# A megakernel of a dynamic filter and a bidirectional Mamba block: TensorE's products of the scan path are placed one phase earlier in its order, and a gated product one scan later

## The chip, the core and the metric

One core of a Trainium2 chip runs the whole program in one launch. The metric is device time in microseconds (us); lower is better. All data is fp32 except for a few small bf16 selections.

The engines are called as in the profile: PE is TensorE (matmul), PEld its weight loads, DVE is VectorE, ACT is ScalarE, POOL is GpSimd and SP is SyncE, which here only issues DMAs.

## The reference, cut to what matters

Eight images of 64 channels and 128 x 128 pixels pass through two layers.

```python
# layer 0, "front": a filter of 3 x 3 taps predicted for each pixel
h = leaky_relu(conv3x3(x, w1) + b1)
w_lp = softmax(conv1x1(h, w2) + b2, axis=1)          # 9 weights a pixel
x = x + sum_k shift_k(x) * (delta_center - w_lp)[k]
# layer 1
x_norm = layernorm(x);  seq = layernorm(x_norm as 16384 tokens of 64);  res = seq
for l in range(2):                                    # two bidirectional Mamba blocks
    xin, z = in_proj(rmsnorm(seq))                    # 128 channels each
    for d in (forward, backward):
        u  = silu(causal_conv1d(xin)); dt = softplus(dt_proj(x_proj(u)))
        h_t = exp(dt * A) * h_{t-1} + dt * u * B      # 128 channels x 16 states
        y_d = sum_n(C * h) + D * u
    seq = seq + out_proj((y_f + y_b) * silu(z))
# "mix"
x = x + dwconv(conv1x1(x_norm)) * (conv3x3(rmsnorm(seq)) + res)
# "ffn"
g1, g2 = dwconv(conv1x1(layernorm(x)))                # 170 channels each
x = x + conv1x1(gelu(g1) * g2)
```

## The kernel before, in words

The selective scan is the long part: 128 channels x 16 states = 2048 independent recurrences over 16384 tokens, twice (two directions) for each of two layers and eight images. A **chunk** is 1024 tokens of one direction of one layer of one image; a chunk has U = 16 scan **steps**, each of which does the recurrence of 128 rows (32 channels x 4 states) over 1024 tokens. 8 images x 64 chunks x 16 steps make 8192 scans, which run one after the other on DVE. For each of these steps:

- POOL forms `bu` = (dt x u) x B for two steps at a time (`drive`, L991, three buffers).
- ACT forms the decay exp(dt x A) in PSUM, two steps ahead (`decay`, L999, tile `w`, two buffers).
- DVE scans (`scan`, L1017 and L1019) and, in about two thirds of the steps, multiplies by C (`product`, L1041); in the others POOL does (L1038).
- ACT saves the last column as the next chunk's start (`keep`, L1031), and PE sums the states into `y` (`collect`, L1050 and L1057, one buffer).

The work that feeds a chunk runs one to two chunks ahead, as methods of the class `Chunk`; PE's part of it is what the text calls the **main path's products**: `conv` (L869, tile `xp`, read by ACT L875 into `xc`), `gate` (L884, `zp`, ACT L892), `step` (L910, `dp`, ACT L917 into `dt`), `bc` (L928, `bcp`, ACT L935), and after a backward-and-forward pair `project` (L1086 and L1089, `op`), a norm's `means` (L405, `ms`) and `spread` (L420, `rb`, read by DVE L1103 in `normed`). All of them write one PSUM tag, `mm`, with one buffer: each has to wait until the one before it has been read.

Beside the scans run, spread over the steps, the three per-image stages `Front`, `Mix` and `Ffn` (the **side work**), with PSUM tags `bg` and `acc` of one buffer each. While one image's 1024 steps run, steps 0 to 180 or so have the Mix of the image before beside them, 180 to 569 its Ffn, and 569 to 1024 the Front of the next image. After the last scan comes the last image's Ffn, alone.

The order of every engine's instructions is written out by hand. Each method is filed under a pair (time in steps, phase), and the pairs are worked off in sorted order, methods of one pair in the order in which they were filed, chunks before Front, Mix and Ffn. A method issues its instructions on its engine's queue there and then, and each engine goes through its queue in that order.

```python
FEED, SCAN, MID, PROD, DECAY, REST = range(6)
def at(time, phase, fn, *args):
    steps.setdefault((time, phase), []).append((fn, args))
...
for key in sorted(steps):
    for fn, args in steps[key]:
        fn(*args)
```

So inside one step FEED comes first, then the scan, its product, then DECAY (where all evacuations of PSUM stand) and at last REST (where most of PE's side work stands). A main path product filed under FEED of step t follows all that is filed under REST of step t-1.

In Ffn, `gelus` (L763 for `gt`, L765 for `ga`, on ACT) is filed at a + 11 under REST; a table load for gelu goes ahead of it and one for exp follows it. `rest_times` (L768, DVE) multiplies `gt` by the other half in PSUM.

Of the kernel before, what the change touches and what calls it, by code (L numbers as in the profile page):

```python
# [36 lines left out]
FEED, SCAN, MID, PROD, DECAY, REST = range(6)  # L37
# [18 lines left out]
def kernel(ctx: ExitStack, tc: tile.TileContext, a: dict, out: bass.AP):  # L56
# [123 lines left out]
    with tc.tile_pool(name="wspill", bufs=1) as fp, tc.tile_pool(name="wprep", bufs=2) as pp, \  # L180
# [98 lines left out]
        for l in range(DEPTH):  # L279
# [17 lines left out]
            for d in range(2):  # L297
                cw = pp.tile([DI, KC], F32, tag="cw", name="cw")
                nc.sync.dma_start(cw, a["L1_conv_conv_w"][l, d])
                for j in range(KC):  # L300
                    t = turned(inx2, diagonal(cw[:, j : j + 1], DI), P, DI)
                    at = j if d == 0 else KC - 1 - j
# [51 lines left out]
    def at(time, phase, fn, *args):  # L354
        steps.setdefault((time, phase), []).append((fn, args))
# [349 lines left out]
    class Ffn:  # L705
# [92 lines left out]
        def plan(self, a):  # L798
            early = 12 if self.alone else 0
            at(a - 4 - early, REST, self.load, 0)  # L800
            at(a - 3 - early, REST, self.load, 1)

            if self.alone:
                groups = ((0, 0, self.first_out, 2), (3, 2, None, 0), (6, 1, self.times, 9))
                gelus, out = 5, 12
            else:
                groups = ((0, 0, self.first_out, 5), (6, 2, None, 0), (14, 1, self.times, 19))
                gelus, out = GELU, 19
            for t, g, end, to in groups:
                for i in range(4):  # L810
                    at(a + t + (0 if self.alone else i), REST, self.conv, g, i)
                for h in range(2 if end else 0):
                    at(a + to, DECAY, end, h)
            at(a + gelus, REST, self.gelus)
            at(a + gelus + 1, DECAY, self.rest_times)
            at(a + out - 5, REST, self.load_x2)
            at(a + out, REST, self.project)
            at(a + out + 2, DECAY, self.add)
            at(a + out + 2, REST, self.store)
# [15 lines left out]
    class Chunk:  # L835
# [282 lines left out]
        def plan(self):  # L1118
            b = self.t0 - 2 * U
            at(b + 3, REST, self.load_hn)  # L1120
            for h in range(2):
                at(b + 7 + h, FEED, self.conv, h)
                at(b + 7 + h, DECAY, self.conv_out, h)
                if self.second:
                    at(b + 9 + h, FEED, self.gate, h)
                    at(b + 9 + h, DECAY, self.gate_out, h)
                at(b + 14 + h, FEED, self.step, h)
                at(b + 14 + h, DECAY, self.step_out, h)
            at(b + SILU, REST, self.silu)
            at(b + SOFTPLUS, REST, self.softplus)  # L1130
            if self.second:
                at(b + 13, REST, self.store_gate)
            b = self.t0
            at(b - 16, FEED, self.bc)
            at(b - 16, DECAY, self.bc_out)
            at(b - 14, REST, self.store_bc)
            at(b - 13, REST, self.store_dt)
            at(b - 11, FEED, self.dtx)
            at(b - 10, REST, self.store_du)
            j0 = self.pairs[0][0] // 2  # L1140
            at(b - 10, REST, self.load_states, "bp", j0)
            at(b - 8, REST, self.load_channels, "dup", 0)
            at(b - 6, REST, self.load_channels, "dtp", 0)
            at(b - 5, REST, self.load_states, "bp", 1 - j0)
            at(b - 4, REST, self.load_channels, "dup", 1)
            at(b - 4, REST, self.load_states, "cp", j0)
            at(b - 2, REST, self.load_channels, "dtp", 1)
            at(b + 0, REST, self.load_states, "cp", 1 - j0)
            for k in range(U // 2):
                at(b + 2 * k - 5, REST, self.drive, k)  # L1150
                at(b + 2 * k + 3 + (k % 4 == 0), REST, self.collect, k)
            for u in range(U):
                at(b + u - 2, DECAY, self.decay, u)
                at(b + u, SCAN, self.scan, u)
                at(b + u + self.on_pool(u), FEED if self.on_pool(u) else PROD, self.product, u)
            for h in range(2):
                if self.second:
                    at(b + 8 * h + 1, REST, self.load_yf, h)
                    at(b + 8 * h + 6, REST, self.add_yf)
                    at(b + 8 * h + 7, REST, self.load_gate, h)  # L1160
                if self.second:
                    at(b + 8 * h + 12, FEED, self.y_out, h)
                else:
                    at(b + 8 * h + 11, DECAY, self.y_out, h)
                    at(b + 8 * h + 12, REST, self.store_y, h)
            if not self.second:
                return
            b += U
            n = self.norm
            at(b + 2, REST, self.load_h)  # L1170
            at(b + 5, FEED, self.project)
            at(b + 6, DECAY, self.residual)
            at(b + 6, DECAY, self.square)
            if self.l == 0:
                at(b + 7, REST, self.store_h)
            at(b + 12, FEED, lambda: n.means(mm_tile, self.sq))
            at(b + 13, DECAY, n.means_out)
            at(b + 14, REST, n.root)
            at(b + 17, FEED, n.spread, mm_tile)
            at(b + 18, DECAY, self.normed)  # L1180
            if self.l:
                at(b + 19, DECAY, self.weighted)
            at(b + 19, REST, self.store_hn)
# [7 lines left out]
    for b in range(B):  # L1191
        a, last = IMAGE * b, b == B - 1
# [36 lines left out]
```

## Time and profile before

| | us |
|---|---|
| median of 3 timed runs (30005.71 to 30014.66) | 30010.1 |
| time of the profiled execution | 29956.31 |
| its span from first to last instruction | 29954.4 |
| before the first scan | 579.7 |
| from the first scan's start to the last scan's end | 28757.6 |
| after the last scan | 617.2 |

Mean granted TensorE clock over the span: 0.881. The fourth image's 1024 steps, cut into the three stretches in which Mix, Ffn and Front stand beside the scans (busy time of each engine, from the table by stage):

| stretch (us from the span's start) | us | PE | DVE | ACT | POOL | granted clock |
|---|---|---|---|---|---|---|
| 11417.10 to 12044.00, Mix | 626.90 | 519.94 | 577.58 | 385.87 | 601.53 | 0.88 |
| 12044.00 to 13385.40, Ffn | 1341.40 | 1126.44 | 1258.54 | 878.22 | 1261.76 | 0.91 |
| 13385.40 to 15029.70, Front | 1644.30 | 1350.96 | 1539.39 | 1054.05 | 1601.07 | 0.88 |

Idle time of an engine is the stretch less its busy time. The list of waits puts the idle time just ahead of an instruction down to what released it: "who <- whom: us in total, times, longest us". In the timeline a line is: start, length, engine, line of the kernel, operation, tiles, shape, count, and in brackets the idle time before it and its releaser.

### The profile page before, as it was taken

How to read it: one execution, taken by the hardware profiler on the slowest of the kernel's cores; microseconds unless marked ns; L12 is line 12 of the kernel's file. 1: busy time of each engine (PE TensorE's matmuls, PEld its weight loads, DVE VectorE, ACT ScalarE, POOL GpSimd, SP SyncE). 2: the span in 40 equal slices, each digit the busy share in tenths (PEclk: the TensorE clock that was granted, in tenths of full speed). 3: DMA queues.
4: the chain of work that ended last, by engine and by line, in shares of the span. 5: the costliest groups of instructions: out<-in, count | busy, mean ns of one | idle time of the engine just before them, and what ended most of it. 6: DMA issues, size and time to landing. Idle time of an engine off the chain costs nothing. (4 is left out here: it accounts for less than half of the span.)

```text
span 29954.4 us, 307972 instructions
## 1 busy us (share of the span) xinstructions
PE 24257.7 (81%) x96344; PEld 8093.1 (27%) x96344; DVE 27086.6 (90%) x17258; ACT 18533.8 (62%) x28316; POOL 27661.8 (92%) x8732
## 2 busy tenths in 40 slices
PE   7666888878888788887888788887888878888579
PEld 3211232223322233222322223222232223322123
DVE  3899999999999999999999999999999999999992
ACT  2566666666666666666666666666666666666661
POOL 3999999999999999999999999999999999999991
PEclk8777888988989888988899889898898988889789
DMA  4776676766777677776777767776677766777672
GB/s 100 210 241 214 221 235 230 237 213 223 237 231 237 213 225 237 232 232 210 233 232 238 225 214 232 232 237 223 215 236 232 240 214 222 235 234 234 214 240 75
DMA packets 2529698, 6617.29 MB, mean 221 GB/s; under 512 B 417862, under 2 KB 722262, under 8 KB 2525750
## 3 DMA queue, kind: packets, MB, share of 16 engines
q1 hardware_dynamic: 2528054, 6597.59, 68.4%
q8 instruction: 761, 12.47, 0.2%
q14 instruction: 883, 7.23, 0.1%
HBM read 5363.40 MB, written 1266.10 MB: 221 GB/s over the span
## 5 line engine op out<-in xcount | busy, mean ns | idle before, releaser
L991 POOL TENSOR_TENSOR bu<-dup,bp 128x2048 f32<-128x2048 f32 x4096 | 18578.8, 4539 | 557.7 <-DVE w L1019 421.4
L999 ACT ACTIVATE w<-dtp,a_neg 128x1024 f32<-128x1024 f32 x8192 | 9162.3, 1118 | 510.2 <-DVE hs L1017 313.9
L1038 POOL TENSOR_TENSOR hs<-hs,cp 128x1024 f32<-128x1024 f32 x2832 | 6685.3, 2361 | 197.9 <-ACT state L1031 133.3
L1041 DVE TENSOR_TENSOR hs<-w,cp 128x1024 f32<-128x1024 f32 x5360 | 6564.9, 1225 | 310.9 <-DMA cp<-bc_dram 77.6
L1017 DVE TENSOR_TENSOR_SCAN w<-w,state,bu 128x1024 f32<-128x1024 f32 x2677 | 6280.9, 2346 | 346.5 <-ACT w L999 345.9
L1019 DVE TENSOR_TENSOR_SCAN w<-w,state,bu 128x1024 f32<-128x1024 f32 x2683 | 6291.0, 2345 | 314.1 <-ACT w L999 313.5
L1057 PE MATMUL y<-hs,sel_y 128*32 128x512 f32 x32768 | 5183.3, 702 | 33.0 <-POOL hs L1038 32.6
L1031 ACT COPY state<-w 128x1 f32<-128x1 f32 x5360 | 837.4, 156 | 5040.0 <-DVE hs L1041 5004.5
L1017 DVE TENSOR_TENSOR_SCAN hs<-w,state,bu 128x1024 f32<-128x1024 f32 x1419 | 3321.3, 2341 | 86.4 <-ACT w L999 36.9
L1019 DVE TENSOR_TENSOR_SCAN hs<-w,state,bu 128x1024 f32<-128x1024 f32 x1413 | 3307.7, 2341 | 52.8 <-ACT w L999 34.7
L1050 PE MATMUL y<-xc,dskip 128*64 128x512 f32 x4096 | 1622.3, 860 | 2025.6 <-ACT yv L1074 1339.3
L869 PE MATMUL xp<-hn,wx 128*128 128x512 f32 x4096 | 2269.2, 682 | 485.3 <-ACT xc L875 339.8
L746 PE MATMUL fp<-fw,bgw 128*128 128x512 f32 (+1 forms) x6144 | 2353.9, 638 | 64.7 <-ACT ga L759 63.5
L1057 PEld LDWEIGHTS y<-hs,sel_y 128*32 128x32 f32 x32768 | 736.8, 116 | 3496.6 <-issue 2469.7
L1031 ACT COPY state<-hs 128x1 f32<-128x1 f32 x2832 | 540.2, 191 | 1829.2 <-DVE hs L1019 929.6
L414 POOL TENSOR_TENSOR r<-r,neg_half 128x8 f32<-128x8 f32 x768 | 1263.5, 1645 | 380.5 <-ACT r L411 323.9
L875 ACT ACTIVATE xc<-xp,cbias 128x512 f32<-128x512 f32 x1024 | 697.2, 681 | 1415.1 <-PE xp L869 1414.7
L910 PE MATMUL dp<-xc,wdt 128*128 128x512 f32 x2048 | 1228.5, 684 | 351.8 <-ACT dt L917 268.2
L752 PE MATMUL fp<-fw,bgw 64*128 64x512 f32 (+1 forms) x6144 | 1501.1, 608 | 0.0
L999 ACT ACT_TABLE_LOAD x1134 | 1454.9, 1283 | 20.1
L947 POOL TENSOR_TENSOR dt<-dt,xc 128x1024 f32<-128x1024 f32 x512 | 1212.8, 2369 | 246.5 <-DMA dt_dram<-dt 223.8
L510 PE MATMUL acc<-t,ident 128*128 128x512 f32 x2304 | 1361.3, 675 | 0.0
(184 smaller groups left out, 26903.7 us busy)
## 6 DMA issues: line engine op xcount, KB each, us to landing
bp<-bc_dram SPq DMA_DIRECT2D x4096, 256.0 KB, 4.0
dup<-du_dram SPq DMA_DIRECT2D x4096, 256.0 KB, 5.0
dtp<-dt_dram SPq DMA_DIRECT2D x4096, 256.0 KB, 5.0
cp<-bc_dram SPq DMA_DIRECT2D x4096, 256.0 KB, 5.0
hn<-hn_dram SPq DMA_DIRECT2D x1024, 256.5 KB, 4.8
dt_dram<-dt SPq DMA_DIRECT2D x512, 512.0 KB, 3.1
du_dram<-dt SPq DMA_DIRECT2D x512, 512.0 KB, 2.6
yf_dram<-yv SPq DMA_DIRECT2D x512, 256.0 KB, 4.4
```

The costliest lines, as they stand in the source:

```text
L746: nc.tensor.matmul(o, wpair[:, i, g, m], self.win[h][:, i : i + ROWS, 0:W], start=(i == 0), stop=False)
L752: nc.tensor.matmul(o, wlast[rows, i, g, m], self.win[h][rows, i : i + ROWS, lo : W + lo], start=False, stop=(i == 2),)
L869: nc.tensor.matmul(self.xp[h], wx[:, self.l, self.d, i, :], self.hn2[:, s.start + 2 * i : s.stop + 2 * i], start=(i == 0), stop=(i == 1),)
L991: nc.gpsimd.tensor_tensor(bu, self.dup[self.pairs[k][1]], self.over_pair("bp", k), ALU.mult)
L999: nc.scalar.activation(w, self.dtp[gp][:, i, :], AF.Exp, scale=a_neg[:, self.l, self.d, g, j : j + 1])
L1017: nc.vector.tensor_tensor_scan(to, w, bu, s0, ALU.mult, ALU.add)
L1019: nc.vector.tensor_tensor_scan(to[:, ::-1], w[:, ::-1], bu[:, ::-1], s0, ALU.mult, ALU.add)
L1031: nc.scalar.copy(self.column(u), h[:, T - 1 : T] if self.d == 0 else h[:, 0:1])
L1038: nc.gpsimd.tensor_tensor(hs, hs, c, ALU.mult)
L1041: nc.vector.tensor_tensor(hs, w, c, ALU.mult)
L1050: nc.tensor.matmul(self.y[C * h : C * h + C, :], dskip[:, self.l, self.d, C * gp : C * gp + C], self.xc[:, s], start=True, stop=False,)
L1057: nc.tensor.matmul(self.y[lo : lo + 32, :], sel_y, hs[:, i, s], start=False, stop=(k % 4 == 3))
```

## The change

Every main path product goes from FEED of step t to REST of step t-1. Within REST of one step chunks are filed first, so these products then stand on PE ahead of the Front, Mix and Ffn products of REST of step t-1, and no longer behind them; `project` also passes the `collect` of the following chunk that opens a new `y`. What is filed under DECAY (all reads of these products) stays. `dtx` and `y_out`, on POOL and DVE, stay under FEED. `rest_times` goes from DECAY of the step after the gelus to MID of the step after that: behind one more scan. While the last image's Ffn runs alone, there is no scan between, and DVE's order is the same there.

The order of the instructions changes on PE, and on DVE in 112 places (seven images x 16 tiles), where `gt` L768 and the scan that followed it change places. On ACT, POOL and SP it stays the same, instruction for instruction.

```diff
@@ Ffn.plan
             at(a + gelus, REST, self.gelus)
-            at(a + gelus + 1, DECAY, self.rest_times)
+            at(a + gelus + 2, MID, self.rest_times)
@@ Chunk.plan
             b = self.t0 - 2 * U
             at(b + 3, REST, self.load_hn)
             for h in range(2):
-                at(b + 7 + h, FEED, self.conv, h)
+                at(b + 6 + h, REST, self.conv, h)
                 at(b + 7 + h, DECAY, self.conv_out, h)
                 if self.second:
-                    at(b + 9 + h, FEED, self.gate, h)
+                    at(b + 8 + h, REST, self.gate, h)
                     at(b + 9 + h, DECAY, self.gate_out, h)
-                at(b + 14 + h, FEED, self.step, h)
+                at(b + 13 + h, REST, self.step, h)
                 at(b + 14 + h, DECAY, self.step_out, h)
...
             b = self.t0
-            at(b - 16, FEED, self.bc)
+            at(b - 17, REST, self.bc)
             at(b - 16, DECAY, self.bc_out)
...
             b += U
             at(b + 2, REST, self.load_h)
-            at(b + 5, FEED, self.project)
+            at(b + 4, REST, self.project)
             at(b + 6, DECAY, self.residual)
             at(b + 6, DECAY, self.square)
...
-            at(b + 12, FEED, lambda: n.means(mm_tile, self.sq))
+            at(b + 11, REST, lambda: n.means(mm_tile, self.sq))
             at(b + 13, DECAY, n.means_out)
             at(b + 14, REST, n.root)
-            at(b + 17, FEED, n.spread, mm_tile)
+            at(b + 16, REST, n.spread, mm_tile)
             at(b + 18, DECAY, self.normed)
```

## The prediction

> **What bounds the kernel now.** The page's busy line first:
>
> ```profile
> PE 24257.7 (81%) x96344; PEld 8093.1 (27%) x96344; DVE 27086.6 (90%) x17258; ACT 18533.8 (62%) x28316; POOL 27661.8 (92%) x8732
> ```
>
> POOL and DVE are both nearly full, so the question is which of the two waits for the other. In DVE's list of waits, taken up to the end of the last scan (29337 us), no row has POOL's `bu` as releaser:
>
> ```profile
> DVE w L1017 <- ACT w L999: 345.9, 302, 3.2
> DVE hc L529 <- PE rb L420: 321.8, 127, 15.7
> DVE w L1019 <- ACT w L999: 313.5, 193, 3.2
> DVE t L504 <- PE wb L500: 199.7, 103, 11.1
> DVE gt L768 <- ACT gt L763: 171.8, 107, 2.2
> DVE hn L561 <- PE rb L420: 141.7, 70, 14.4
> DVE hn L1103 <- PE rb L420: 134.7, 79, 3.7
> ```
>
> POOL does wait for DVE (`bu` <- DVE w L1019 421.4 us, L1017 116.3 us), and in the timeline of the fourth image its `bu` ends on average 4 to 11 us before its scan starts. DVE sets the pace, POOL follows with little to spare: by the table by stage its idle time per image is 25.4 us beside Mix, 79.6 beside Ffn and 43.2 beside Front, 148 in all. A microsecond that DVE no longer waits is time, as long as POOL keeps up.
>
> DVE waits for ACT's decay, though ACT is busy for 62%. ACT's list says why:
>
> ```profile
> ACT xc L875 <- PE xp L869: 1414.7, 634, 18.3
> ...
> ACT dt L917 <- PE dp L910: 526.8, 294, 4.6
> ACT bc L935 <- PE bcp L928: 509.5, 249, 3.8
> ```
>
> ACT works in order; while it waits for a main path product, the next decay stands behind. One such place in the timeline (step 11 of a chunk, beside Ffn):
>
> ```profile
> 12383.97 1.98 PE L869 MATMUL xp<-hn,wx 128*128 128x512 f32 x4
> ...
> 12385.99 0.69 ACT L875 ACTIVATE xc<-xp,cbias 128x512 f32<-128x512 f32 x1 [3.04 <-PE xp L869]
> ...
> 12386.61 1.13 ACT L999 ACTIVATE w<-dtp,a_neg 128x1024 f32<-128x1024 f32 x1
> ...
> 12387.78 2.36 DVE L1019 TENSOR_TENSOR_SCAN w<-w,state,bu 128x1024 f32<-128x1024 f32 x1 [2.39 <-ACT w L999]
> ```
>
> PE was late because eight Ffn products (12382.05, 1.99 us) stood ahead of xp; the buffer had been free since 12381.85. And the gelu wait:
>
> ```profile
> 9629.52 0.69 DVE L768 TENSOR_TENSOR gt<-gt,fp 128x512 f32<-128x512 f32 x1 [1.52 <-ACT gt L763]
> ...
> 9631.88 1.12 ACT L999 ACTIVATE w<-dtp,a_neg 128x1024 f32<-128x1024 f32 x1
> ...
> 9633.65 2.34 DVE L1019 TENSOR_TENSOR_SCAN hs<-w,state,bu 128x1024 f32<-128x1024 f32 x1
> ```
>
> **Part A, the gated product.** 112 times `gt` goes behind a scan of 2.35 us. DVE waits 171.8 us there now (the page's 528.4 less 356.6 in the tail, where order and wait stay), at most 2.2 us at a time, so the scan covers it; its own decay is ready in every case. Next is late the scan after that: its decay stands on ACT behind the gelus and a table load, ends at 9633.00 in the rows above and was needed at 9633.65. This margin of 0.65 us is the same at nearly all 112 places, so if ACT's times stay, only min(wait, 0.6) is won, summed 60 us. ACT comes to the gelus after a `conv_out` or `step_out` that waits for PE (2.78 us in this example); where part B takes 1 us of that away, the whole 172 us is won. I take 140, with ends 60 and 172. What queues behind the later `gt` is one product L1041, 0.7 us later; its PSUM buffer is next written 7 us after (9637.42).
>
> **Part B, main path products earlier.** No instruction is added, no DMA moves, SP's and POOL's queues are passed by nothing. 2590 us of ACT's idle time stand before reads of these products (the three rows above and 140.6 for `gate`), but only what reaches DVE counts. DVE's rows with ACT w as releaser are 345.9 + 313.5 + 36.9 + 34.7 = 731 us. I went through them by step: step 11 alone has 195 us beside Ffn, 163 beside Front and 67 beside Mix, with 2.1 to 2.9 us of ACT waiting for xp just before each; with the places behind xp, dp, bcp and zp elsewhere they come to 640 us. The other 90 follow table loads and stay. Put first, a product starts when the reader of the one before it is done: of the 3840 moved products 2292 pass something on PE, and for these the old start less the time at which buffer and PE were both free is 1.2 to 2.6 us by kind, against waits of 0.7 to 2.9 us. I take 85% of 640: 545 us won, with ends 320 (half) and 640. `spread` is also earlier beside Front, where 81 of L1103's 134.7 us lie: 65 won. `project` passes dskip and its `collect`; both wait for the same read of `y`, so `collect` comes later by its three products (some 1.3 us). DVE waits for PE's y 26 us in all, and three buffers of `hs` cover it: 0, at most 30.
>
> **Part C, side work later.** Side products that are passed come later by 1.1 us (dp, zp, bcp, rb) or 1.85 (xp), and by the time PE stands waiting for the mm buffer (0.1 us a product beside Ffn, up to 1.2 beside Front). Beside Ffn nobody is near: 581 conv groups have two steps until they are read. Beside Front readers come one step later: `weight` to `t` L504, `spread` to L529 and L561. There 406 `weight` are passed with margins of 0 to 1.5 us (mean 0.9), which gives 200 us of new DVE wait; 189 spreads with 0 to 0.7, 130 us (at 14261.69 `hc` waits 1.68 us for an rb that ends as it starts: margin none, and dp of 1.12 us will stand ahead of it); logits, centered and the rest 75. With 42 us beside Mix and 17 at the start that is 460 us, each counted as if alone. A delay hides the one right after it in the same tile, so I take 60%: 280 us lost; ends 140 and 500.
>
> **The sum.** 140 + 545 + 65 - 280 = 470 us of DVE waiting less, 59 an image. POOL's 148 us an image leave room, but little beside Mix and Front, and the next in line are DMA waits (L1041 <- cp, 77.6 us) and POOL's own waits for r (L414, 323.9 us), which get no better. I count two thirds: 310 us. The profiled execution goes from 29956.3 to 29646; the median of the runs lies 54 us above its time, so 30010 - 310 = **29700**.
>
> **The clock.** Granted clock is 0.88, 0.91 and 0.88 in the three stretches, and the stalls I put in front of products are mostly 1.2 us or less, so the sum has no term for it. The Trainium skill (TensorE: Matmul & The Clock Gate, section "Why this matters for your kernels") speaks against such stalls: idle gaps of TensorE above some 3 us halve its clock. [...] No row before shows it for this order.
>
> **The rivals.**
> *Head of line.* PE meets a main path product whose buffer is not read yet and stands, with all side work behind it. Place: Front, steps 13 to 0 and 6 to 9. It decides once the mean delay of a passed Front product exceeds its margin by over 1.2 us: some 600 passed weights and spreads then cost 700 us, the rest 100, against 560 won where ACT's times improve less (A 60, B 500): slower by 240, 30250. For it: PE is busy 82% beside Front and idles in between for DVE's t (413 us). Against: conv and bc have mean stalls of 0.8 and 1.2 us at most, and PE gets back what ACT no longer delays.
> *POOL takes over.* Beside Front and Mix POOL has only 69 us an image to give; if half of it is no use, what is won is Ffn's part alone, 140 + 210 less what Front loses net, some 130 to 200 us: 29840.
> *Nothing to see.* B's gain and C's loss cancel and A gives 60: 29950 to 30070, about the 0.2% (60 us) that a measurement of this kernel can tell from no change. That the change does not do what it says is ruled out by the order of the instructions, which does move.
>
> **How the numbers follow.** Forecast, 180 to 500 us won: 0.50. POOL or another next wait, 60 to 180: 0.20. More than 500, ACT's waits gone entirely and C small: 0.08. Within 60 us: 0.08. Head of line, slower: 0.14. So faster 0.78, same 0.08, slower 0.14. The range leaves out the best few hundredths (ends 172 + 640 + 80 - 140 = 750, two thirds of it 500 to 560) and most of head of line: 29450 to 30090.
>
> **What would show it.** Right: ACT's xc <- xp falls below 500 us and dt, bc to a third; DVE's w <- ACT w from 731 to under 200; gt <- ACT gt to near 0 before 29337 us, with 356 left in the tail; Front's hc, hn L561 and t rows grow by some 280 together; Ffn's stretch shortens most, by 35 to 45 us an image; POOL's idle time shrinks in all. Wrong: ACT's rows stay (PE late for want of time, not of order), or DVE's rows for rb and wb grow by more than its rows for ACT w shrink, or Front's stretch gets longer by over 60 us an image.

## The result, and the profile after

| | before | after |
|---|---|---|
| median, us (range, runs) | 30007.9 (29990.17 to 30015.59, 6) | 30125.97 (30104.24 to 30152.06, 6) |
| time of the profiled execution | 29956.31 | 30118.27 |
| its span | 29954.4 | 30116.5 |

The ratio is 1.0043 [1.0032, 1.0053]: slower by 0.43%, 118 us between the medians and 162 us between the profiled spans. The forecast was 29700, with 30090 as the upper end of its range; sign and range were wrong.

The busy line of the page after:

```profile
PE 24494.9 (81%) x96344; PEld 8218.4 (27%) x96344; DVE 27092.6 (90%) x17258; ACT 18592.8 (62%) x28316; POOL 27658.7 (92%) x8732
```

DVE and POOL are busy as long as before, to within 6 us; with the same counts of instructions PE's sum has grown by 237 us and ACT's by 59. The time is therefore idle time on DVE and POOL, and the table by stage (the fourth image again: Mix, Ffn, Front; columns as in the table of before) tells beside what:

```profile
11511.40:12133.70 622.30, 511.88 (x1907) 183.78 (x1905) 576.85 (x332) 387.36 (x579) 600.54 (x188) 0.89 0.73 233
12133.70:13455.80 1322.10, 1129.14 (x4513) 336.95 (x4514) 1256.28 (x749) 879.16 (x1287) 1261.55 (x366) 0.91 0.73 237
13455.80:15143.20 1687.40, 1376.58 (x5599) 491.30 (x5600) 1542.83 (x1049) 1058.44 (x1672) 1601.59 (x542) 0.86 0.68 217
```

Cutting every image at its scans 180 and 569 gives these means, each over seven stretches: Ffn 1340.9 to 1322.0 us, Mix 621.6 to 623.0, Front 1646.4 to 1685.3. Seven times these differences are -132, +10 and +272 us; with 12 us in the rest that is the 162 us. So the change does one thing beside Ffn and the opposite beside Front, and the rest of this document asks why.

DVE's list of waits up to the end of the last scan (29499 us):

```profile
DVE hc L529 <- PE rb L420: 456.5, 221, 15.2
DVE t L504 <- PE wb L500: 413.6, 234, 10.7
DVE hn L561 <- PE rb L420: 257.0, 123, 4.9
DVE w L1017 <- ACT w L999: 193.3, 217, 1.3
DVE mx L466 <- PE lp L460: 177.9, 75, 52.2
DVE w L1019 <- ACT w L999: 137.3, 136, 1.4
DVE hs L1041 <- DMA cp<-bc_dram: 103.3, 22, 9.0
DVE hs L1019 <- issue: 61.4, 46, 1.8
DVE hs L1017 <- PE y L1057: 59.2, 27, 5.9
DVE hn L1103 <- PE rb L420: 50.0, 52, 3.0
```

The two rows for ACT's decay went from 659 to 331 us, and L1103 from 134.7 to 50.0: the change does what it says. But `hc`, `t` and `hn` L561, which read Front's side products, went from 663 to 1127 us, and the gelu wait is gone from this part of the list. ACT's list shows the same from its side; before these rows had 1414.7 and 509.5:

```profile
ACT xc L875 <- PE xp L869: 639.6, 367, 20.4
ACT bc L935 <- PE bcp L928: 277.4, 183, 5.8
```

### The profile page after: what moved, and what is told of

It is laid out like the page before. It is cut to its first block, busy times and chain, and to the rows that moved or that the text cites. A ratio compares the mean times of both kernels' runs of the same rounds, so it can differ in the third digit from the quotient of the medians.

```text
span 30116.5 us, 307965 instructions
## 1 busy us (share of the span) xinstructions
PE 24494.9 (81%) x96344; PEld 8218.4 (27%) x96344; DVE 27092.6 (90%) x17258; ACT 18592.8 (62%) x28316; POOL 27658.7 (92%) x8732
## 5 line engine op out<-in xcount | busy, mean ns | idle before, releaser
L1057 PE MATMUL y<-hs,sel_y 128*32 128x512 f32 x32768 | 5042.3, 690 | 35.3 <-POOL hs L1038 35.0
L869 PE MATMUL xp<-hn,wx 128*128 128x512 f32 x4096 | 2379.1, 710 | 1051.5 <-ACT xc L875 747.1
L1050 PE MATMUL y<-xc,dskip 128*64 128x512 f32 x4096 | 1560.1, 833 | 1425.6 <-ACT yv L1074 1285.5
L910 PE MATMUL dp<-xc,wdt 128*128 128x512 f32 x2048 | 1250.8, 695 | 688.5 <-ACT dt L917 450.9
L869 PEld LDWEIGHTS xp<-hn,wx 128*128 128x128 f32 x4096 | 815.2, 217 | 2437.0 <-ACT xc L875 1094.4
L510 PE MATMUL acc<-t,ident 128*128 128x512 f32 x2304 | 1444.6, 718 | 0.0
```

What stands on the lines that cost most here:

```text
L510: nc.tensor.matmul(self.acc, ident, self.t.pop(k), start=False, stop=(k == 8))
L869: nc.tensor.matmul(self.xp[h], wx[:, self.l, self.d, i, :], self.hn2[:, s.start + 2 * i : s.stop + 2 * i], start=(i == 0), stop=(i == 1),)
L1050: nc.tensor.matmul(self.y[C * h : C * h + C, :], dskip[:, self.l, self.d, C * gp : C * gp + C], self.xc[:, s], start=True, stop=False,)
L1057: nc.tensor.matmul(self.y[lo : lo + 32, :], sel_y, hs[:, i, s], start=False, stop=(k % 4 == 3))
```

## The experiments

`Front`, `Mix` and `Ffn` below are mean us of an image's stretch from the profiled execution. The ratio is against the kernel before on the same chip (its medians there were 29993.8 to 30008.1). Where an edit holds only beside Front, this helper decides by the step:

```python
def beside_front_at(t):
    r = t % IMAGE
    return (FRONT_AT - FRONT_STEP <= r < FRONT_AT + NCH * FRONT_STEP + 26
            and t < (B - 1) * IMAGE) or t < FIRST_FRONT_AT + NCH * FRONT_STEP + 26
```

| kernel | median us | ratio, 95% | Front | Ffn | Mix |
|---|---|---|---|---|---|
| before (profiled) | | | 1646.4 | 1340.9 | 621.6 |
| after (profiled) | 30126.0 | 1.0043 [1.0032, 1.0053] | 1685.3 | 1322.0 | 623.0 |
| gate_only | 29980.5 | 0.9992 [0.9983, 1.0001] | 1645.3 | 1339.3 | 625.5 |
| products_only | 30179.8 | 1.0060 [1.0048, 1.0073] | 1685.5 | 1329.4 | 622.3 |
| old_beside_front | 29862.3 | 0.9955 [0.9941, 0.9968] | 1646.0 | 1321.6 | 623.3 |
| new_beside_front_only | 30217.3 | 1.0071 [1.0058, 1.0084] | 1681.1 | 1343.8 | 617.5 |
| front_conv_new | 29914.7 | 0.9973 [0.9962, 0.9985] | 1651.5 | 1323.6 | 622.2 |
| front_step_bc_new | 30143.4 | 1.0048 [1.0036, 1.0061] | 1679.6 | 1322.3 | 625.8 |
| front_gate_norm_new | 29963.4 | 0.9988 [0.9979, 0.9997] | 1656.9 | 1323.1 | 625.2 |
| early_evacuation | 30070.0 | 1.0023 [1.0013, 1.0032] | 1645.0 | 1364.3 | 617.0 |
| one_step_side_first_2 | 29923.6 | 0.9972 [0.9961, 0.9983] | 1651.2 | 1334.8 | 616.8 |
| first_halves_new | 30119.3 | 1.0041 [1.0028, 1.0055] | 1683.6 | 1323.6 | 622.1 |
| step_first_only | 30088.8 | 1.0027 [1.0017, 1.0037] | 1676.3 | 1323.8 | 623.6 |
| all_but_step_first | 30019.3 | 1.0008 [0.9999, 1.0017] | 1663.7 | 1322.8 | 623.7 |
| spreads_ahead | 30136.3 | 1.0040 [1.0027, 1.0053] | 1681.3 | 1324.4 | 623.8 |
| front_early_and_first | 30278.5 | 1.0092 [1.0078, 1.0106] | 1711.1 | 1322.2 | 617.8 |
| step_first_r_early | 30098.0 | 1.0031 [1.0019, 1.0043] | 1676.3 | 1324.3 | 623.8 |
| mix_early | 29815.7 | 0.9938 [0.9926, 0.9951] | 1646.4 | 1323.4 | 615.8 |

The second table is DVE's idle time in the seven Front stretches, in us, by what ended it (from the trace; `w` takes in every wait for ACT's decay). Most verdicts rest on it.

| kernel | hc | hn L561 | t | mx | hn L1103 | w | other | sum |
|---|---|---|---|---|---|---|---|---|
| before | 110 | 101 | 37 | 0 | 81 | 277 | 144 | 749 |
| old_beside_front | 122 | 101 | 42 | 0 | 69 | 276 | 135 | 746 |
| after | 152 | 224 | 249 | 75 | 3 | 132 | 159 | 995 |
| front_conv_new | 145 | 121 | 124 | 3 | 82 | 180 | 127 | 781 |
| front_step_bc_new | 175 | 181 | 92 | 48 | 81 | 243 | 141 | 961 |
| front_gate_norm_new | 79 | 152 | 133 | 0 | 21 | 268 | 167 | 821 |
| step_first_only | 194 | 151 | 62 | 0 | 117 | 283 | 138 | 946 |
| all_but_step_first | 89 | 204 | 206 | 58 | 2 | 128 | 164 | 851 |
| first_halves_new | 160 | 116 | 198 | 5 | 41 | 327 | 143 | 990 |
| spreads_ahead | 103 | 191 | 298 | 90 | 1 | 127 | 156 | 967 |
| early_evacuation | 164 | 102 | 126 | 5 | 0 | 197 | 141 | 736 |
| one_step_side_first_2 | 108 | 158 | 17 | 0 | 76 | 267 | 158 | 783 |
| front_early_and_first | 99 | 40 | 119 | 0 | 42 | 744 | 137 | 1181 |

**The parts, and the places.** Four kernels: each part alone, and the moved products with before's places either beside Front or everywhere else.

```diff
# gate_only: before with
-            at(a + gelus + 1, DECAY, self.rest_times)
+            at(a + gelus + 2, MID, self.rest_times)
# products_only: the whole change without that line
# old_beside_front: the whole change, and for every moved product
-                at(b + 6 + h, REST, self.conv, h)
+                feed(b + 7 + h, self.conv, h)   # FEED of that step beside Front, else REST of the step before
# new_beside_front_only: before with feed() the other way round
```

> The gated product alone is moved (behind one more scan); all TensorE products stay where they were before. Theory S (the loss is made beside Front, by side products that now stand behind main path products; both parts win beside Ffn): only the Ffn stretches get shorter, by 5 to 12 us an image (1341 to about 1332), Front stays at 1645 us; total -40 to -90 us against before, about 29940. Rival P (beside Ffn POOL sets the limit as soon as DVE's gelu wait is gone): the Ffn stretch goes all the way to the changed kernel's 1323 us, about -130 us in total, and the earlier products add nothing there.

> TensorE's main path products alone are moved; the gated product stays where it was before. Theory S: Front stretches as in the changed kernel (1685 against 1645 us an image, +280 us in total), Ffn stretches shorter by 8 to 15 us an image (about 1330); total +160 to +220 against before, about 30200. Rival P: the Ffn stretch is no shorter than before, 1341, since the gelu wait still stands; total +270 to +290.

> The whole change, except that products which fall beside a Front keep their old place (FEED). Theory S: Front stretches fall back to 1645 us, Ffn stays at 1323, Mix about 622; total about -130 us against before, 29880. Rival C (the lower granted TensorE clock, 0.874 against 0.881, is the cause of the loss and comes from the new order as such): the clock stays near 0.875 and a Front stretch stays above 1665; total not below before.

> Only products that fall beside a Front go to their new place; everything else, the gated product included, as before. Theory S: Front stretches 1685 us, all others as before (Ffn 1341); total +270 to +290 us, about 30290. Rival P or C: if the loss comes from POOL or the clock in other stretches as well, Front's growth alone gives less, under +150 us.

The gated product alone gives nothing that can be told from no change: 28 us, where theory S had 40 to 90 and rival P 130. Beside the seven Ffns `gt`'s own wait fell from 172 us to 0, but waits of other scans came in its place; in DVE's list of gate_only up to the last scan stands a row that was not in before's:

```profile
DVE hs L1019 <- issue: 124.0, 78, 1.8
```

("issue": the profile shows no releaser.) Together with the moved products it is worth more: 1329.4 to 1322.0 us an Ffn, 54 us between the medians of products_only and after. The products alone came out as theory S forecast, Front 1685.5 and Ffn 1329.4.

The places split cleanly. With before's places beside Front, Front is back at 1646.0 us while Ffn keeps 1321.6, and the run beats before and after alike, by 0.45%. With the new places beside Front alone, Front has nearly the whole loss (1681.1), though the run lost 209 us and not the 270 to 290 of the forecast. So the loss is made beside Front, by the order there; the clock or POOL in other stretches (rivals C and P) are not needed for it.

**Which kind of product.** Beside Front one kind at a time in its new place, the rest as in old_beside_front.

```diff
 def feed(t, kind, fn, *args):
-    if not beside_front_at(t):
+    if not beside_front_at(t) or kind == 'conv':                  # front_conv_new
+    if not beside_front_at(t) or kind in ('step', 'bc'):          # front_step_bc_new
+    if not beside_front_at(t) or kind in ('gate', 'project', 'means', 'spread'):   # front_gate_norm_new
         at(t - 1, REST, fn, *args)
```

> As old_beside_front, but conv (xp) takes its new place beside Front too. Theory K (it goes by kind: a product pays where its lateness held up ACT's decay, and costs where a side product with one step of margin stands behind it): conv is what held up the decay of step 11 (163 us of DVE wait beside Front), and the weights behind it have margin; Front 1638 us an image against 1646, total about 29810. Rival L (it goes by length: the longest product, 1.85 us, costs most): Front 1660 or more, total 29960 or more.

> As old_beside_front, but step and bc (dp, bcp) take their new place beside Front too. Theory K: little was waiting for them, and logits, spreads and weights behind them have little margin: Front 1663 us an image, total about 29980. Rival L: three products of 1.1 us, cost as conv's two of 1.85: Front about 1660, so this run alone tells little; the three together do.

> As old_beside_front, but gate, project, means and spread take their new place beside Front too; only Fronts beside second directions (15 of some 28 chunks) have any. Theory K: the spread wins 78 us of DVE wait (hn L1103), gate next to nothing, and both push weights and spreads of Front back: Front 1668 us an image, total about 30010. Rival L: fewer and shorter products than the others: Front under 1655.

Against 1646.0 they cost 5.5, 33.6 and 10.9 us an image, together 50 where the whole costs 39. Neither theory had this order: K forecast 1638, 1663 and 1668, and L had conv, the longest, as the dearest. conv pays for itself nearly: `w` falls by 96 us, `t` grows by 82. step and bc win 33 us of `w` and lose 231 on `hc`, `hn` L561, `t` and `mx`. Row by row the kinds add up: these four readers grow by 128, 231 and 99 us, 458 together, and by 435 in the whole change; `w` falls by 96, 33 and 8, 137 together, against 144. What does not add is L1103 (up 13 and 12, down 48 by kinds; down 66 in the whole change).

**Standing, or standing behind.** Two remedies, and a split by where PE stands.

```diff
# early_evacuation: the whole change with, for conv, gate, step and bc
-                at(b + 7 + h, DECAY, self.conv_out, h)
+                at(b + 7 + h, FEED, self.conv_out, h)
# one_step_side_first_2: the whole change with REST, then MAIN, then LATE
-                at(b + 6 + h, REST, self.conv, h)
+                at(b + 6 + h, MAIN, self.conv, h)      # and the other six moved products
-                at(t + 13, REST, self.gather, k)
+                at(t + 13, LATE, self.gather, k)       # hidden, Mix's and Ffn's taps and add_h too
# first_halves_new: old_beside_front with
+    if not beside_front_at(t) or kind in ('conv0', 'step0', 'project', 'means', 'spread'):
```

> The whole change, but ACT's evacuations of conv, gate, step and bc (conv_out, gate_out, step_out, bc_out) stand under FEED of their step instead of DECAY: ahead of that step's decay on ACT's queue, so that the one mm buffer is read about one decay (1 to 2 us) sooner. With the whole change Front's stretch took 1685 us an image (before 1646). Theory H (head of line: the loss comes from PE standing at a moved product until ACT has read the mm buffer before it, with all side products of the step queued behind): the stalls xp<-ACT xc, bcp<-ACT dt and dp<-ACT dt shrink to under half and Front falls to 1665 us or less, the run to 29,980 or less. Theory L (length: the loss is the running time of the moved products, which the side products now wait out): the products are as long as ever, Front stays at 1675 to 1690 us, the run at 30,060 to 30,170. Both expect a cost of up to 10 us an image in each stretch from the decays, which now stand behind the evacuations.

> The whole change, but inside REST of a step there are three groups on PE: first the side products that are read within a step (logits, spreads, weights, means, centered, pointwise), then the moved main path products, then hidden, gather, the taps of Mix and Ffn and add_h, whose readers stand several steps later. Theory S (Front lost because products read within a step stand behind the main path's; whether by their length or by PE's standing does not matter here): Front comes back from 1685 us an image to 1655 or less, Ffn stays near 1322, the run is at 29,920 or less, and the waits hn L561<-PE rb and t L504<-PE wb fall back to within a third of before's. Rival D (displacement: somebody has to stand behind the main path's products, and gather's late end holds the sums just as much, through t's buffers and hc): Front 1665 to 1685, run 29,990 to 30,120, with t<-PE wb and hc<-PE rb still at twice before's.

> The whole change beside Mix and Ffn; beside Front only the products in whose new place PE stands little: the first halves of conv and step, project, means and spread. The second halves of conv and step, both halves of gate and bc, which follow another mm product by one step or less and whose new place is the one where PE waits for ACT's evacuation, stand beside Front where they stood before. By the waits of PE in one Front stretch of the changed kernel the moved first halves hold 37 us of standing (dp<-ACT r 23.2, xp<-ACT sq 14.1), the second halves and bc 128 us (xp<-ACT xc 58.2, bcp<-ACT dt 36.1, dp<-ACT dt 30.3, zp<-ACT gate 3.1) against 30 us before. Theory H: three quarters of the 39 us an image come back, Front 1650 to 1658 us, the run 29,890 to 29,950. Theory L (length): about half of the products stand as in the changed kernel, so that half comes back or less, Front 1662 to 1675, the run 29,975 to 30,065.

Both remedies take the loss beside Front away, 1645.0 and 1651.2 us.

early_evacuation did beside Front what theory H forecast (1665 or less), and not what theory L did (1675 to 1690). It leaves the order and the length of PE's products as they are; what changes is how long PE stands at a moved product until ACT has read the buffer. PE's list of waits in the fourth Front, first before:

```profile
PE xp L869 <- ACT xc L875: 15.3, 4, 5.8
PE dp L910 <- ACT dt L917: 8.5, 6, 2.6
PE bcp L928 <- ACT dt L917: 5.1, 4, 2.4
```

Then after:

```profile
PE xp L869 <- ACT xc L875: 58.2, 23, 6.2
PE bcp L928 <- ACT dt L917: 36.1, 16, 5.4
PE dp L910 <- ACT dt L917: 30.3, 17, 3.1
```

Then early_evacuation:

```profile
PE xp L869 <- ACT xc L875: 4.7, 2, 2.6
PE dp L910 <- ACT dt L917: 2.2, 4, 0.8
PE bcp L928 <- ACT dt L917: 1.8, 4, 0.9
```

In all seven Fronts these three rows together are 203, 874 and 64 us. The columns of the four readers (`hc`, `hn` L561, `t`, `mx`) are 248, 700 and 397 us: of the 452 us that the change added, 303 went with the standing. L1103 and part of `w` keep what they had won (0 and 197 us), so DVE's idle time is back at 736 us. The run as a whole stayed above H's 29,980, because early_evacuation pays beside Ffn, 1364.3 against 1322.0 us: the decays now stand behind the evacuations (`w` beside the seven Ffns some 360 us against 109).

one_step_side_first_2 wins nothing beside Front (`w` 267, `t` back to 17): a product that stands behind the readers of one step is no earlier than before. It shows that the loss goes through side products read within a step, and rival D fell. It cannot tell length from standing, since both are gone (the three rows are 232 us). Two of its forecasts failed: `hn` L561 stayed at 158 us, and Ffn took 1334.8 and not 1322.

first_halves_new went against both theories: nearly nothing came back, although the second halves and bc stand where they stood before. The second table says how. Against after, `hn`, `t` and `mx` fell by 229 us, but `w` rose by 195 and L1103 by 38: what the second halves had cost the side products, they had won for the decays. What this kernel and front_step_bc_new, the dearest of the kinds, have in common is one moved product, the first half of step.

**One product.**

```diff
# step_first_only: old_beside_front with
+    if not beside_front_at(t) or kind == 'step0':
# all_but_step_first: old_beside_front with
+    if not beside_front_at(t) or kind != 'step0':
# spreads_ahead: the whole change with a phase AHEAD between DECAY and REST
-            at(a + 28, REST, n1.spread, bg_tile)
+            at(a + 28, AHEAD, n1.spread, bg_tile)      # n2 and n3 too
# front_early_and_first: both remedies beside Front and Mix, the whole change beside Ffn
```

> The whole change beside Mix and Ffn; beside Front every main path product stands where it stood before, except the first half of step (dp of h = 0), which stands in its new place. Theory F (the first half of step is the culprit: new place at step 13 of 16, where Front's spreads n1 and n2 stand half of the times, and there PE stands up to 3 us for r L411 of the norm's means, the mm buffer ahead): Front 1665 to 1685 us an image, run 29,995 to 30,135, hc L529<-PE rb at step 14 of 16 about 100 us in seven Fronts against 49 before. Rival T (it takes several products together, none carries it alone): Front 1646 to 1655, run 29,860 to 29,930.

> The whole change, but beside Front the first half of step stands where it stood before. Theory F: Front 1650 to 1660 us an image (what the kinds conv and gate with the norms cost by themselves, 5 and 11 us), run 29,890 to 29,960. Rival T: Front 1672 to 1685, run 30,040 to 30,135.

> The whole change, but Front's three spreads (n1, n2, n3) stand in a phase of their own between DECAY and REST: on PE ahead of the moved products of the same step, and ahead of everything else of REST. Logits, weights, means, centered and pointwise stay behind them. Theory F and theory S (the loss goes through side products read within a step) both expect hc L529<-PE rb and hn L561<-PE rb to fall from 152 and 224 us in seven Fronts to 80 and 120 or less; if the spreads carry most of the loss, Front falls to 1650 to 1662 and the run to 29,875 to 29,960. If weights and logits carry it (t L504 and mx L466 grew by 287 us, the spreads' rows by 166), Front stays at 1668 to 1680 and the run at 30,000 to 30,090.

> The whole change beside Ffn; beside Front and Mix both remedies: evacuations under FEED, and the moved products behind the side products that are read within a step (hidden, gather, Mix's taps and add_h behind them). Each remedy alone brought Front from 1685 to 1645 and 1651 us. If they mend different waits (the early evacuation the moved products' own standing, the other order the side products behind), they add: Front 1610 to 1635, Mix 612 to 617, run 29,570 to 29,800. If both mend the same wait, Front is 1640 to 1651 and the run 29,820 to 29,900.

One product a chunk, 28 of them beside a Front, costs 30.3 us an image: 1.08 us each. Its `w` did not fall at all (283 against 276): a pure loss. And the three rows of PE's standing are nearly as small as before (219 us in seven Fronts); only its standing ahead of dp for `r` has grown, from 11 us in old_beside_front to 129, and early_evacuation leaves that one as it is (156, in after 160). So this loss is not the one that early_evacuation took away. The other products together cost 17.7, with 809 us in those rows. Theory F held for its first kernel, for the second only halfway (1663.7, between both forecasts). The delays add here too: the four readers grow by 142 and 292 us, 434 against 435 in the whole change. That 30 and 18 us make 39 and not 48 is again mostly L1103: 48 us later in one kernel and 67 earlier in the other, 66 earlier with both.

How part of the 30 us comes about is seen in the timeline at one of these places, step 13 of a chunk, at the same scan in both kernels (start, length, engine, line, operation, tiles, shape, count, idle time before it). In these kernels L432 is before's L420 (`spread`), L541 its L529, L922 its L910. First old_beside_front:

```profile
3454.12 1.09 PE L432 MATMUL rb<-ident,r 128*64 128x128 f32 x16
3455.15 1.12 PE L922 MATMUL dp<-xc,wdt 128*128 128x512 f32 x2
3455.26 0.69 DVE L541 TENSOR_TENSOR hc<-hc,rb 128x512 f32<-128x512 f32 x1 [1.68 <-PE rb L432]
```

Then step_first_only:

```profile
3469.59 1.12 PE L922 MATMUL dp<-xc,wdt 128*128 128x512 f32 x2
3470.65 1.09 PE L432 MATMUL rb<-ident,r 128*64 128x128 f32 x16
3471.79 0.69 DVE L541 TENSOR_TENSOR hc<-hc,rb 128x512 f32<-128x512 f32 x1 [2.73 <-PE rb L432]
```

The spread had no margin, `hc` already waited for it, and the product's 1.05 us go into DVE's wait to the hundredth: 1.68 to 2.73. PE does not stand here. A second kind of place is like this one, step_first_only again:

```profile
3588.85 2.08 PE L922 MATMUL dp<-xc,wdt 128*128 128x512 f32 x2 [3.05 <-ACT r L423]
3590.86 1.97 PE L432 MATMUL rb<-ident,r 128*64 128x128 f32 x16
...
3592.88 0.69 DVE L541 TENSOR_TENSOR hc<-hc,rb 128x512 f32<-128x512 f32 x1 [1.87 <-PE rb L432]
```

Here PE stood 3.05 us, and both products took 1.8 times as long as in the rows above. The standing itself adds little here, though. In old_beside_front PE is idle ahead of the same spread as well, and the spread is as slow; it was just in time:

```profile
3570.69 1.97 PE L432 MATMUL rb<-ident,r 128*64 128x128 f32 x16 [2.64 <-POOL r L426]
...
3573.18 0.66 DVE L541 TENSOR_TENSOR hc<-hc,rb 128x512 f32<-128x512 f32 x1
```

Counted from DVE's `t` just before, the spread ends 2.42 us later than there, and 2.08 of it is the product's own length at that speed. At the speed of the first place it would have been 1.1, so nearly half of the price here is the slow speed.

These two kinds of place are not all. DVE's instructions have the same order in both kernels, so their waits can be compared one by one. Where the product stands right ahead of a spread for `hc`, DVE waits 85 us more in the seven Fronts, 39 of them at places of the second kind. Another 50 us stand at `hn` L561 and 48 at `hn` L1103, where other products stand ahead; how the delay gets there is not shown.

spreads_ahead moved the loss instead of mending it. Both theories had `hc` at 80 us and `hn` L561 at 120 or less; `hc` fell from 152 to 103 us, `hn` only from 224 to 191, and `t` rose from 249 to 298: at step 14 alone, by the trace, from 9 to 131, for the weights of step 13 now stand behind the spread and the product both. front_early_and_first went against both forecasts, at 1711.1: the evacuations stand ahead of the decays on ACT and wait for products that come late again (ACT's idle time before reads of xp, dp, zp and bcp is 2256 us in seven Fronts, 463 in after), and `w` rose to 744 us. The remedies exclude each other.

**Is it the standing after all?** One more kernel for step_first_only's second kind of place, and one for the best version.

```diff
# step_first_r_early: step_first_only with
-            at(b + 13, DECAY, n.means_out)
+            at(b + 13, FEED if beside_front_at(b + 13) else DECAY, n.means_out)
# mix_early: old_beside_front with, for conv, gate, step and bc beside Mix
-                at(b + 7 + h, DECAY, self.conv_out, h)
+                at(b + 7 + h, FEED, self.conv_out, h)
```

> step_first_only (beside Front only the first half of step is in its new place), and beside Front ACT's reading of the norm's means (means_out, tile r, step 13 of 16) stands under FEED, ahead of that step's decay, instead of DECAY. That frees the mm buffer about a decay (1.1 us) or more sooner. In step_first_only PE stood 129 us at dp<-ACT r in seven Fronts, and Front took 1676.2 us an image against 1646.0 in old_beside_front. Theory H (PE's standing, with Front's products queued behind it): the standing falls to 40 us or less, hc L529<-PE rb and hn L561<-PE rb come back from 194 and 151 to about 122 and 101, Front is at 1646 to 1657 and the run at 29,860 to 29,950. Rival W (the place: one more product ahead of the spreads, whether it stands or not): the standing falls all the same, Front stays at 1668 to 1680, the run at 30,010 to 30,100.

> old_beside_front (the whole change, with before's places beside Front), and beside Mix alone ACT's evacuations of conv, gate, step and bc stand under FEED, ahead of the decay. In early_evacuation Mix took 617.0 us an image against 623.0 with the whole change. Expected: Mix 617, the rest as in old_beside_front, run 29,800 to 29,840. Rival: what Mix gains is lost in the next stretch, run 29,850 to 29,875.

Front stayed at 1676.3, but the edit did not do what it was made for. At the two places shown ACT read `r` earlier by 0.34 and 0.05 us, counted from DVE's product before it, not by a decay, since ACT's queue had itself waited for DVE at that step, and PE's standing ahead of dp was 121 us (73 of it now put down to ACT's `state`) where it had been 129. This experiment is inconclusive; that for the first half of step it is the length, more than the standing, rests on the timeline at the places shown alone.

mix_early came out as expected: 29815.7 us, 0.9938 [0.9926, 0.9951], the fastest version, Mix 615.8 with Front and Ffn unchanged. Beside Mix the early evacuation helps, beside Ffn it cost 42 us.

## Why the prediction was wrong

**What bounds the kernel** was read rightly: DVE sets the pace, and POOL follows. DVE's idle time turned into time at a rate of one, or a little more: beside Front it grew by 246 us and the stretches by 272; beside Ffn it fell by 113 and the stretches by 132. POOL cannot win a loss back: beside Front it is busy for 95 to 97% of the stretch, and it waits in its turn for the late scan. But the "two thirds" was also to cover the waits that are next in line, and these took more: beside Ffn `gt` and `w` gave up some 300 us, of which 113 were left, as DVE then waited for POOL's `bu` (47 us), for `ga` L771 (31), with no releaser shown ("issue", 61) and more elsewhere.

**Part A, 140 us:** mis-sized. The 172 us of `gt`'s wait did go; the tail alone is left, 359.4 us in DVE's list. Alone it gave 28 us (interval of the ratio up to 1.0001), with part B 54. The lower end, 60, was nearer. The text had named the reason, the scan after the next one with its margin of 0.65 us, and then let part B remove it; part B removed some.

**Part B, 545 + 65 us:** the mechanism held, the 85% did not. `w` fell from 277 to 132 us beside the seven Fronts and from 238 to 109 beside the Ffns, about a half each, and up to the last scan from 731 to 331, by 400 and not 545. ACT's wait for xp fell to 640 us and not below 500: a product that stands first still waits for the one buffer, and ACT for it. L1103's 81 us beside Front went to 3, as forecast.

**Part C, 280 us: the step that failed.** Its gross list was good. It gave 405 us beside Front: 200 for weights, 130 for spreads, 75 for the rest; `t` grew by 212, `hc` and `hn` L561 by 165, `mx` by 75. Its allowance for PE's standing, up to 1.2 us a product, is about what the trace of after shows (1.2 for conv and bc, 1.0 for step). It quoted a spread with no margin and the 1.12 us of dp that would stand ahead of it, and that is one of the places found in the trace. The error was mostly the 60%, on the grounds that one delay hides the next. The four readers of Front's products (`hc`, `hn` L561, `t`, `mx`) went from 248 to 700 us: 452 more, over the gross sum instead of 60% of it. The experiments by kind test that assumption between kinds: 458 us singly, 435 together, so 5% is hidden and not 40%. Within one kind it was not tested.

So beside Front the sum should have been: won 145 (`w`) and 78 (L1103), lost 452 and 15 of the rest, a net loss of 244 us of DVE's waiting. By the prediction's terms it was a gain of some 30 (an estimate: 545 us by `w`'s share beside Front, 277 of 731, and 65, less 60% of 405). Beside Ffn, where 35 to 45 us an image were forecast, 19 were won.

Up to the last scan DVE's waits add up like this: `gt` won 169 us (forecast 140), the decays 400 (545), L1103 85 (65), the four readers lost 571 (280), and other rows 236 more. That is 153 us lost instead of 470 won. Part C is the largest miss, but with it alone put right the sum would still have shown 179 us won; the decays and the new waits took the rest.

**The clock.** The prediction had no term for it, as stalls would be 1.2 us or less. They were longer: dp waited up to 3.7 us for `r`, and in such places products took 2.07 us instead of 1.13. The Trainium skill (TensorE: Matmul & The Clock Gate, section "Why this matters for your kernels") states that gaps above some 3 us halve TensorE's clock, and one row above agrees, 3.05 us ahead of 2.08; another lies below that figure, 2.64 us ahead of a spread of 1.97 us instead of 1.09. The mean granted clock beside Front fell from 0.876 to 0.859 and PE's busy time rose by 27 us an image. But this does not order the kernels: early_evacuation has 0.861 and Front at 1645.0, all_but_step_first 0.871 and 1663.7. The clock makes single places dearer and does not explain the loss alone; how much of the loss is slow products was not separated.

**The rivals.** Head of line gave the right sign, the right stretch and steps 13 to 0, at a chance of 0.14, and its price of 240 us was twice what the medians show. Its mechanism was right for the larger part: PE stands at products whose buffer is not read yet, with side work behind, and 303 of the 452 us went when early_evacuation took that standing away. At the costliest single product, the first half of step, the places shown speak for the product's length. "POOL takes over" is refuted beside Front, since POOL's idle time beside Front rose from 317 to 587 us. Of the signs named, "rows for rb and wb grow by more than its rows for ACT w shrink" came true (464, or 379 with L1103, against 329); "Front longer by over 60 us" did not, at 39.

**What stays open:** which of the four evacuations gives early_evacuation its relief, and whether part of it is only moved, as its `w` is 65 us above after's. And how the delay from the first half of step reaches `hn` L561 and L1103.

## What to carry to other kernels

When a product is moved ahead in an engine's queue, list what it passes together with the time until that is read; where the reader already waits, the price is the full length of what now stands in front, and here next to nothing came off for delays that fall together. Add the time that the moved product itself stands for its buffer: here that was the larger part. Judge such a move separately for each kind of work that it passes: here the same move of products won 12 us beside one stage (19 with the gated product) and lost 39 beside another, and the version that makes it only where the readers are far is 0.45% faster than before. A wait that ends in another place of the same in-order chain (a gelu's, here) is won only as far as the next instruction of that chain has margin.

## What the hardware showed beyond that

How long PE may be idle before its products slow down can be read from the 1024 pairs of dp in one profile. By the idle time of PE just before, the share of pairs that took over 1.8 us (1.13 otherwise) was, in after's trace: up to 1.5 us idle, 1 to 6%; 1.5 to 2 us, 21%; 2 to 2.5 us, 40%; above that, 64%. So an idle time of 2 us is already a risk here. But the idle time just before does not decide alone: in the trace of before none of the 36 pairs after 1.5 to 2 us was slow, and 9 of the 15 after up to 0.5 us were; a gap further back may be the reason. In the trace of before 57 pairs stood behind 2 us or more, in that of after 144.
